# A graph layer's node windows sized by their place in the sorted edges, with fifteen segments in place of thirty-three

## The chip, the cores and the metric

The kernel runs on one core of a Trainium2 chip. The metric is the device time of one execution in microseconds (us). The engines are named as in the profile: PE (TensorE matmul, with PEld for its weight loads), DVE (VectorE), ACT (ScalarE), POOL (GpSimd) and SP (SyncE, which here issues DMAs only). Times inside an execution are given in us from the start of its span.

## What is computed

One message-passing layer over 12,500 nodes of 48 features and 400,000 edges of 32 features, sorted by destination:

```python
h = jnp.maximum(_layernorm(x, axis=-1), 0.0)
x_i = h[dst]
x_j = h[src]
tmp = jnp.concatenate([x_i, x_j, edge_attr], axis=1)
hid = jax.nn.relu(tmp @ W1 + b1)
msg = hid @ W2 + b2
out = jax.ops.segment_sum(msg, dst, num_segments=12500)
return x + out
```

`W1` is 128 by 128, `W2` is 128 by 48, all in float32. `dst` is drawn as 12500 times the square of a uniform number and then sorted, so the low nodes have many edges each and the high nodes few: a run of 1,024 edges covers few nodes at the start and some tens at the end.

## The kernel before

**Tables first.** `node_tables` (up to about 75 us) normalises the nodes and multiplies them by the two node parts of `W1`. It writes `tab_a` (for destinations) and `tab_b` (for sources) to DRAM and leaves the normalised rows turned in `ht`. It also computes a flag that sends the kernel to another path, `general`, if the edges of some chunk cover too many nodes; with these inputs the path is `windows`.

**Chunks.** `windows` walks the edges in 391 chunks of 8 tiles of 128 edges. The nodes of a chunk lie in a window that starts at the chunk's first destination and is `W` = 80 nodes wide. For chunk c:

- `prepare(c)`: SP loads the edge features into rows 80 to 111 of `lhs`, the destinations broadcast to 80 partitions (`row`), and 80 rows of `tab_a` (`rhs`). POOL gathers the source rows of `tab_b` into `gb` by one indirect DMA for each tile, for those tiles that come in no other way. DVE compares `row` with the window's node numbers, which fills rows 0 to 79 of `lhs` with a 0/1 matrix and sums the degrees into `deg` (L379).
- `columns(c, part)`: some tiles come as columns. A turned copy of the source table (`bt`) is kept in SBUF, and DVE (71) and ACT (72) copy one 128x1 column for each edge into `gt` (L348), at addresses that are loaded into registers (L272).
- `rows`: 15 rows for each chunk come into `gs` by small DMAs of SP (L289).
- `compare(c)`: DVE makes the 0/1 matrix `hot`, 128 edges by 8 tiles by 80 nodes (L389).
- `before(c)` multiplies `lhs` with `rhs` into `pre` (L400); `gathered(c)` adds the source rows to it (L421); `hidden(c)` is the relu on ACT (L437).
- `fold(c)` multiplies `hid` with `hot` into `p_g`, 8 tiles one after another (L445), and turns the degrees (L448); `add(c)` adds `p_g` into the running segment `seg` at the window's place (L460).

The first four chunks have their source rows gathered from x itself (`xg`), so POOL's gathers into `gb` start with chunk 4. Of a chunk's eight tiles POOL gathers 7 as a rule, sometimes 6: 2,618 gathers in all.

**Segments.** `seg` is one of two buffers of 1,024 nodes. Twelve chunks share a segment (`GQ`; the first has four, and the last three). At a segment's end `segment_next` clears the other buffer (L476, two memsets) and copies the overlap of 80 nodes into it (L478, SBUF to SBUF). In the chunks that follow, `segment_sum` multiplies the old segment by `W2` and `b2` in two halves of 512 nodes (L488, L489), `segment_add` adds them to `xseg` (L495), and `segment_store` writes it (L499).

**Order.** All engines run a hand-written order (`manual_schedule`): in round c the loop does `prepare(c)`, `before(c-1)`, `fold(c-2)`, `add(c-2)`, `compare(c)`, `gathered(c-1)`, `hidden(c-1)`, with `columns` in between and the segment's work near the end of the round. POOL has nothing but its gathers in this loop. It runs ahead of the others until `gb` has no free buffer: the pool `gp` has 7, and a chunk's buffer comes free when PE has read it in L421.

Of the kernel before, what the change touches and what calls it, by code (L numbers as in the profile page):

```python
# [8 lines left out]
F32 = mybir.dt.float32  # L9
I32 = mybir.dt.int32  # L10
AF = mybir.ActivationFunctionType
ALU = mybir.AluOpType
# [30 lines left out]
RAW_PART = 16  # L43
HALF = (W - 1) / 2
K = W + DE
# [27 lines left out]
BT0 = 16512  # L73
SEG0 = 161696
SEG_SIZE = 8 * L
# [154 lines left out]
def windows(nc, tc, gp, bt, ident, idx, raw, rhss, x_t, tab_a, tab_b, dst, edge_t, w2s, b2s,  # L230
# [5 lines left out]
    with ExitStack() as es:  # L236
# [15 lines left out]
        wnum = ps_w.tile([P, W], F32, name="wnum")  # L252
        nc.vector.tensor_scalar_add(wnum, wrow, -HALF)

# [8 lines left out]
        def group(c):  # L263

            return divmod(c + OFF, GQ)

        def begin(g):
            return max(0, g * GQ - OFF)

# [55 lines left out]
        def columns(c, part):  # L325
# [15 lines left out]
            for k, of in enumerate(got[:n]):  # L341
# [6 lines left out]
                copy(gts[j][:, e : e + 1], bt8[:, bass.ds(of, 4)].bitcast(F32))  # L348

        def prepare(c):  # L350
            n = min(T, NT - c * T)
            at = c * CE
            lhs = ld.tile([P, CE], F32, name="lhs")
# [10 lines left out]
            nc.sync.dma_start(  # L364
                rhs.bitcast(U8)[:W, :],
                taba8[bass.ds(base, 4 * HID * W)].rearrange("(w h) -> w h", w=W),
            )
# [11 lines left out]
            nc.vector.tensor_scalar(  # L379
                lhs[:W, : n * P], row[:, : n * P], bw[:, c : c + 1], None,  # L380
                op0=ALU.is_equal, op1=ALU.add, accum_out=deg[:, :1],
            )
            st[c].update(rhs=rhs, lhs=lhs, gb=gb, deg=deg)

        def compare(c):

            n = st[c]["n"]
            hot = wp.tile([P, T, W], F32, name="hot")
            nc.vector.tensor_tensor(  # L389
                hot[:, :n, :], wnum.unsqueeze(1).to_broadcast([P, n, W]),  # L390
                rel[:, c * T : c * T + n].unsqueeze(2).to_broadcast([P, n, W]), op=ALU.is_equal,
            )
            st[c]["hot"] = hot
# [46 lines left out]
        def fold(c):  # L440
            s = st[c]
            n = s["n"]
            p_g = ps_g.tile([HID, 2, W], F32, name="p_g")
            for t in range(n):
                nc.tensor.matmul(  # L445
                    p_g[:, 0, :], s["h"][:, t, :], s["hot"][:, t, :], start=t == 0, stop=t == n - 1
                )
            nc.tensor.matmul(p_g[:, 1, :], s["deg"], ident[:W, :W], start=True, stop=True)  # L448
            s["p_g"] = p_g

        def add(c):

            s = st.pop(c)
# [6 lines left out]
            nc.vector.tensor_add(to, to, s["p_g"])  # L460
# [3 lines left out]
        def segment_load(g):  # L464

            first, = numbers(begin(g), SEG, 1, mybir.EngineType.SP)
            xs[g] = xp.tile([D, L], F32, name="xseg")
            n = L if begin(g + 1) < NCH else END_L
            nc.sync.dma_start(xs[g][:, :n], x_t[:, bass.ds(node(first), n)])

# [26 lines left out]
        def segment_store(g, n):  # L497
            first, = numbers(begin(g), SEG, 1, mybir.EngineType.SP)
            nc.sync.dma_start(out_t[:, bass.ds(node(first), n)], xs.pop(g)[:, :n])  # L499

        with tc.manual_schedule():
            for c in range(NCH + 2):
# [30 lines left out]
                columns(c, 10)  # L533
                if k == GQ - 3 or c == NCH - 1:
# [21 lines left out]
def general(nc, tc, bt, ident, x_t, tab_a, tab_b, src_it, dst_it, dst, edge_t, w1, w2s, b2s,  # L556
            accs, out_t):

    with ExitStack() as es:
# [97 lines left out]
        with tc.tile_pool(name="gfin", bufs=1) as fin, tc.tile_pool(  # L657
            name="g_f", bufs=1, space=PSUM
        ) as ps_f:
            for r0 in range(0, NR, 14):  # L660
                s = slice(r0, r0 + 14)
                got = []
                for k in range(GNACC):
                    a = fin.tile([P, 14, D], F32, name=f"a{k}")
                    nc.sync.dma_start(
# [5 lines left out]
                nc.vector.tensor_add(got[0], got[0], got[2])  # L671
                for r in range(14):
                    p_f = ps_f.tile([D, P], F32, name="p_f")
# [6 lines left out]
def tile_gnn_preln(  # L680
# [63 lines left out]
    for k in range(3):  # L744
        deg = const.tile([W, P], F32, name=f"deg{k}")
        nc.gpsimd.memset(deg, 0.0)
        degs.append(deg)
    gp = ctx.enter_context(tc.tile_pool(name="gp", bufs=7))

    with tc.tile_pool(name="keep", bufs=1) as keep, tc.tile_pool(  # L750
# [14 lines left out]
        def loads():  # L765
# [12 lines left out]
            gather(0, RAW_PART)  # L778
            nc.gpsimd.tensor_scalar_add(b0f, b0f, HALF)
            full = NT // T  # L780
# [18 lines left out]
        def squares():  # L799
            nc.scalar.activation(bt[:, :NT], rel, AF.Square)  # L800

        def sources():

            nc.sync.dma_start(srci[:, FIRST:], src_cols[:, FIRST:])

        furthest = keep.tile([P, 1], F32, name="furthest")
        widest = keep.tile([P, 1], F32, name="widest")
# [3 lines left out]
        def most():  # L811
# [3 lines left out]
            )  # L815
            nc.vector.tensor_scalar(furthest, furthest, HALF * HALF, None, op0=ALU.is_gt)
            nc.vector.tensor_scalar(widest, widest, MID * MID, None, op0=ALU.is_gt)
            nc.vector.tensor_tensor(furthest, furthest, widest, op=ALU.max)

        def check():  # L820
# [6 lines left out]

            nc.vector.tensor_scalar_add(wcol, wcol, -HALF)
            nc.vector.tensor_scalar(bw, b0f[:W, :], wcol[:W, :], None, op0=ALU.add)
# [105 lines left out]
```

## Time and profile before

| | |
|---|---|
| median of three executions | 3366.36 us (3366.21 to 3367.52) |
| the profiled execution's own time | 3372.65 us |
| its span, first to last instruction | 3370.8 us |
| mean granted TensorE clock | 0.911 |
| busy | PE 82%, PEld 64%, DVE 83%, ACT 90%, POOL 75% |
| moved by DMA | 349.24 MB, 104 GB/s in the mean |

The trace's numbers are those of the profiled execution, and sums are made against its span. A line such as "3353.48 0.95 POOL L371 ... [0.30 <-issue]" is a row of the timeline: start, duration, engine, line, operation, operands and count, then the engine's idle time just before and what ended it. In the groups by line, the two numbers behind the bar are the busy time in us and the mean duration in ns, and behind the second bar stands the idle time before these instructions.

### The profile page before, as it was taken

To read this page: it belongs to the slowest core of one execution; us is meant where nothing else is said; L and a number is where in the kernel's file an instruction comes from. 1 tells how busy PE (TensorE), PEld (TensorE's weight loads), DVE (VectorE), ACT (ScalarE), POOL (GpSimd) and SP (SyncE) were. 2 spreads that over 40 slices of the span, in tenths; PEclk is the share of its full clock that TensorE was granted. 3 is DMA by queue.
4 is the path that set the end of the run, shared out by engine and by line. 5 is a ranking of instruction groups with operands and counts; after the bars stand their busy time and mean duration, and the time that the engine had idled before them with its cause. 6 is when DMAs were issued, how large, how long until landed. Compare 5 with 4: busy or idle time off the path is not lost.

```text
span 3370.8 us, 115212 instructions
## 1 busy us (share of the span) xinstructions
PE 2775.6 (82%) x16394; PEld 2158.3 (64%) x16394; DVE 2800.1 (83%) x29140; ACT 3035.6 (90%) x28179; POOL 2530.0 (75%) x2670
## 2 busy tenths in 40 slices
PE   7987778888888888888887788888788788788777
PEld 6666666666666666666666666676666666666565
DVE  6588888888888888888888888888888888888876
ACT  5799998999998999998899999889998999999987
POOL 7677777777777777777777777777777777777776
PEclk9999998998898998988889999888998999899989
DMA  7433333333333333333333333333333333333333
GB/s 262 122 97 104 100 97 100 99 101 100 100 99 100 95 100 102 100 101 97 100 98 101 100 100 102 95 101 97 102 99 98 97 100 98 104 100 97 99 96 83
DMA packets 200234, 349.24 MB, mean 104 GB/s; under 512 B 69219, under 2 KB 107749, under 8 KB 198181
## 3 DMA queue, kind: packets, MB, share of 16 engines
q0 software_dynamic: 84800, 172.53, 18.9%
q1 hardware_dynamic: 114258, 169.09, 16.7%
q14 instruction: 634, 5.19, 0.5%
q8 instruction: 138, 2.26, 0.3%
q10 hardware_dynamic: 404, 0.17, 0.0%
HBM read 322.05 MB, written 22.07 MB: 102 GB/s over the span
## 4 chain that ended last, share of the span: by engine, by line
DVE 71%; issue 14%; PE 5%; DVEq 4%; POOL 2%; DMA 2%; ACT 0%; SPq 0%; POOLq 0%; ACTq 0%
DVE gt L348 47%; DVE lhs L379 12%; DVE hot L389 8%; DVEq L272 4%; DVE seg L460 2%; POOL gb L371 2%; PE pre L400 1%; PE p_g L445 1%; DVE xseg L495 1%; DVE seg L476 1%; DMA row<-in_dst 1%; PE p_f L488 1%; PE p_f L489 1%; DMA gb<-tab_b,srci 1%; PE p_n L195 1%
## 5 line engine op out<-in xcount | busy, mean ns | idle before, releaser
L371 POOL DMA_INDIRECT gb<-tab_b,srci x2618 | 2489.4, 951 | 812.7 <-issue 724.4
L348 ACT COPY gt<-bt 128x1 f32 x27705 | 2618.0, 188 | 63.9 <-issue 54.6
L348 DVE COPY gt<-bt 128x1 f32 x27335 | 1842.1, 144 | 463.3 <-issue 435.1
L400 PEld LDWEIGHTS pre<-rhs,lhs 112*128 112x128 f32 x6250 | 823.5, 208 | 277.1 <-issue 193.4
L400 PE MATMUL pre<-rhs,lhs 112*128 112x128 f32 x6250 | 841.5, 292 | 98.3 <-issue 56.7
L445 PE MATMUL p_g<-hot,hid 128*128 128x80 f32 x6250 | 794.0, 282 | 131.2 <-ACT hid L437 129.1
L445 PEld LDWEIGHTS p_g<-hot,hid 128*128 128x128 f32 x6250 | 758.4, 198 | 164.4 <-ACT hid L437 161.6
L421 PE MATMUL pre<-gb,ident 128*128 128x512 f32 (+2 forms) x1548 | 771.2, 627 | 34.3 <-DMA gb<-tab_b,srci 26.5
L437 ACT ACTIVATE hid<-pre 128x1024 f32<-128x1024 f32 x391 | 397.5, 1017 | 220.2 <-PE pre L421 205.8
L379 DVE TENSOR_SCALAR_CACHE_REDUCE lhs<-row,bw 80x1024 f32<-80x1024 int16 x391 | 494.6, 1265 | 14.8 <-DMA row<-in_dst 14.5
L421 PEld LDWEIGHTS pre<-gb,ident 128*128 128x128 f32 x1548 | 311.8, 225 | 281.0 <-issue 261.7
L421 PE MATMUL pre<-ident,gt 128*128 128x128 f32 x860 | 214.9, 336 | 261.7 <-DVE gt L348 234.7
L421 PEld LDWEIGHTS pre<-ident,gt 128*128 128x128 f32 x860 | 143.8, 210 | 291.5 <-issue 136.4
L389 DVE TENSOR_TENSOR hot<-wnum,rel 128x640 f32<-128x640 f32 x391 | 318.2, 814 | 0.0
L460 DVE TENSOR_TENSOR seg<-seg,p_g 128x160 f32 x391 | 121.5, 311 | 47.8 <-PE p_g L448 47.8
L448 PE MATMUL p_g<-ident,deg 80*128 80x80 f32 x782 | 156.4, 283 | 0.0
L448 PEld LDWEIGHTS p_g<-ident,deg 80*128 80x128 f32 x782 | 123.6, 198 | 0.0
L488 PE MATMUL p_f<-seg,w2s 128*48 128x512 f32 (+1 forms) x134 | 82.2, 700 | 44.3 <-DVE xseg L495 43.9
L489 PE MATMUL p_f<-seg,b2s 1*48 1x512 f32 (+1 forms) x134 | 76.2, 650 | 0.0
L488 PEld LDWEIGHTS p_f<-seg,w2s 128*48 128x48 f32 x134 | 12.3, 135 | 85.9 <-DVE xseg L495 60.0
L476 DVE MEMSET seg<- 128x944 f32 x64 | 54.1, 845 | 9.3
L489 PEld LDWEIGHTS p_f<-seg,b2s 1*48 1x48 f32 x134 | 11.3, 122 | 65.2 <-issue 65.2
(76 smaller groups left out, 429.0 us busy)
## 6 DMA issues: line engine op xcount, KB each, us to landing
gs<-tab_b SPq DMA_DIRECT2D x5760, 0.5 KB
row<-in_dst SPq DMA_DIRECT2D x390, 160.0 KB
lhs<-in_edge_t SPq DMA_DIRECT2D x390, 128.0 KB
gb<-tab_b,srci POOLq DMA_INDIRECT x2618
rhs<-tab_a SPq DMA_DIRECT2D x391, 40.0 KB
xseg<-in_x_t SPq DMA_DIRECT2D x33, 192.0 KB
out_x<-xseg SPq DMA_DIRECT2D x33, 192.0 KB
tab_b<-tab SPq DMA_DIRECT2D x3, 1280.0 KB
```

Source lines behind the costliest of these rows:

```text
L272: return nc.values_load_multi_w_load_instructions(table[c % P : c % P + 1, c // P, at : at + n], engines=[engine], min_val=0, max_val=1 << 23,
L348: copy(gts[j][:, e : e + 1], bt8[:, bass.ds(of, 4)].bitcast(F32))
L371: nc.gpsimd.indirect_dma_start(out=gb[:, t, :], out_offset=None, in_=tab_b[:, :], in_offset=bass.IndirectOffsetOnAxis(ap=srci[:, c * T + t ...
L379: nc.vector.tensor_scalar(lhs[:W, : n * P], row[:, : n * P], bw[:, c : c + 1], None, op0=ALU.is_equal, op1=ALU.add, accum_out=deg[:, :1],)
L389: nc.vector.tensor_tensor(hot[:, :n, :], wnum.unsqueeze(1).to_broadcast([P, n, W]), rel[:, c * T : c * T + n].unsqueeze(2).to_broadcast([P ...
L400: nc.tensor.matmul(pre[:, t, :], s["lhs"][:K, t * P : (t + 1) * P], s["rhs"][:K, :], start=t % BANK == 0, stop=False, skip_group_check=True,)
L421: nc.tensor.matmul(pre[:, t:e, :], lhsT, rhs, start=False, stop=True, skip_group_check=True)
L437: nc.scalar.activation(h[:, :n, :], s["pre"][:, :n, :], AF.Relu)
L445: nc.tensor.matmul(p_g[:, 0, :], s["h"][:, t, :], s["hot"][:, t, :], start=t == 0, stop=t == n - 1)
L448: nc.tensor.matmul(p_g[:, 1, :], s["deg"], ident[:W, :W], start=True, stop=True)
L460: nc.vector.tensor_add(to, to, s["p_g"])
L488: nc.tensor.matmul(p_f[:, :n], w2s, seg[:, 0, s], start=True, stop=False)
```

## The change

The window's width depends on the chunk's place: 16 nodes for chunks 0 to 77, 32 to chunk 164, 48 to 249, 64 to 339, and 80 for the rest. The broadcast of the destinations, the rows of `tab_a`, both comparisons, the columns of `hot` in the fold, the turned degrees and the add into the segment are that wide. `lhs` becomes three fixed buffers whose node rows are cleared once by DVE (and those of `rhs` by POOL), since the matmul L400 still contracts over all 112 rows. Window numbers count from 0 instead of from the window's middle, which removes two small additions of `HALF` (one on POOL), and the check's squares are made in five pieces. `gp` gets 8 buffers. Segments begin at fixed chunks: fifteen of them, the first of 103 chunks, the last of five with a final sum of 400 nodes instead of 320. `xseg` has one buffer and the last segment its own; a segment is stored one round later than before, except the one before the last. The columns stay 71 for DVE and 72 for ACT, and the gathers stay 2,618. The rest of the diff is smaller tiles in `general`.

```diff
-GQ = 12
-OFF = -(NCH - 3) % GQ
+BEGINS = (0, 103, 147, 180, 208, 233, 255, 275, 294, 312, 329, 345, 360, 374, NCH - 5)
-END_L = 4 * W
+END_L = 5 * W
-STORE = 2
+STORE = 3
-HALF = (W - 1) / 2
+SPANS = ((16, 78), (32, 165), (48, 250), (64, 340), (W, NCH))
...
+        lhss = [one.tile([P, CE], F32, name=f"lhs{k}") for k in range(3)]
+        for lhs in lhss:
+            nc.vector.memset(lhs[:W, :], 0.0)
...
+        wh = es.enter_context(tc.tile_pool(name="wh", bufs=2))
-        xp = es.enter_context(tc.tile_pool(name="xp", bufs=2))
+        xp = es.enter_context(tc.tile_pool(name="xp", bufs=1))
...
+        def span(c):
+            return next(w for w, last in SPANS if c < last)
...
             nc.sync.dma_start(
-                row[:, : n * P],
-                dst[at : at + n * P].rearrange("(o e) -> o e", o=1).to_broadcast([W, n * P]),
+                row[:w, : n * P],
+                dst[at : at + n * P].rearrange("(o e) -> o e", o=1).to_broadcast([w, n * P]),
             )
...
             nc.vector.tensor_scalar(
-                lhs[:W, : n * P], row[:, : n * P], bw[:, c : c + 1], None,
-                op0=ALU.is_equal, op1=ALU.add, accum_out=deg[:, :1],
+                lhs[:w, : n * P], row[:w, : n * P], bw[:w, c : c + 1], None,
+                op0=ALU.is_equal, op1=ALU.add, accum_out=deg[:w, :1],
             )
...
-            hot = wp.tile([P, T, W], F32, name="hot")
+            hot = wh.tile([P, T * W], F32, name="hot")
+            hot = hot[:, : T * w].rearrange("p (t w) -> p t w", w=w)
...
-            p_g = ps_g.tile([HID, 2, W], F32, name="p_g")
+            p_g = ps_g.tile([HID, 2 * W], F32, name="p_g")
+            p_g = p_g[:, : 2 * w].rearrange("h (k w) -> h k w", k=2)
...
-            to = segs[k].bitcast(U8)[:, :, bass.ds(at, 4 * W)].bitcast(F32)
+            to = segs[k].bitcast(U8)[:, :, bass.ds(at, 4 * w)].bitcast(F32)
...
-                    if k == GQ - 1:
+                    if c - 1 == begin(g + 1) < NCH:
                         segment_next(g)
...
-                if g > 0 and k == STORE:
+                if g > 0 and k == (STORE if begin(g + 1) < NCH else 2):
                     segment_store(g - 1, L)
...
+    for rhs in rhss:
+        nc.gpsimd.memset(rhs[:W, :], 0.0)
-    gp = ctx.enter_context(tc.tile_pool(name="gp", bufs=7))
+    gp = ctx.enter_context(tc.tile_pool(name="gp", bufs=8))
...
-            nc.gpsimd.tensor_scalar_add(b0f, b0f, HALF)
...
-            nc.scalar.activation(bt[:, :NT], rel, AF.Square)
+            at = 0
+            for k, (w, last) in enumerate(SPANS):
+                to = min(NT, last * T)
+                nc.scalar.activation(
+                    bt[:, at:to], rel[:, at:to], AF.Square,
+                    bias=shift[:, k : k + 1], scale=1.0 / reach(w),
+                )
+                at = to
```

Two places show how instructions move. The first is DVE at the end of the second segment of the kernel before, in the round that adds chunk 15: the add into the segment, then the memsets and the copy of the overlap.

```order
L460 TENSOR_TENSOR seg_635<-seg_635,p_g 128x2x80
L476 MEMSET seg_634 128x944 x2
L272 TENSOR_LOAD last
L478 ISA
L478 COPY seg_634<-seg_635 128x2x80
```

In the change DVE goes from one add straight on to the next columns here, and this group stands 14 times in the program instead of 33 (its first copy without the memsets in both). At the same place:

```order
L471 TENSOR_TENSOR seg_645<-seg_645,p_g 128x2x16
L276 TENSOR_LOAD cols
L352 COPY gt<-bt 128x1 x16
L398 TENSOR_TENSOR hot<-wnum,rel 128x128
L276 TENSOR_LOAD cols
```

The second place is the end of PE's queue in the kernel before, from the source rows of the chunk before the last; `x5` is the last chunk, which has five tiles.

```order
L421 MATMUL pre<-gb,ident 128x384
L488 MATMUL p_f<-seg_634,w2s 48x512
L489 MATMUL p_f<-seg_634,b2s 48x512
L400 MATMUL pre<-rhs_89,lhs 128x128 x5
L445 MATMUL p_g<-hot,hid 128x80 x8
L448 MATMUL p_g<-ident,deg_99 128x80
L421 MATMUL pre<-gb,ident 128x512
L421 MATMUL pre<-gb,ident 128x128
L488 MATMUL p_f<-seg_634,w2s 48x512
L489 MATMUL p_f<-seg_634,b2s 48x512
L445 MATMUL p_g<-hot,hid 128x80 x5
L448 MATMUL p_g<-ident,deg_95 128x80
```

The same stretch of the change has no sums of the segment before the last in it. They stand behind the source rows of the two chunks before, since the last segment now has five chunks:

```order
L430 MATMUL pre<-gb,ident 128x384
L409 MATMUL pre<-rhs_89,lhs_653 128x128 x5
L456 MATMUL p_g<-hot,hid 128x80 x8
L459 MATMUL p_g<-ident,deg_102 128x80
L430 MATMUL pre<-gb,ident 128x512
L430 MATMUL pre<-gb,ident 128x128
L456 MATMUL p_g<-hot,hid 128x80 x5
L459 MATMUL p_g<-ident,deg_98 128x80
```

Behind both stand only the last segment's sums, 320 columns wide before and 400 now.

More of the change, by code (lines that the diff above doesn't have):

```diff
@@ L263, in group @@
         def group(c):
-            return divmod(c + OFF, GQ)
+            g = max(0, sum(first <= c for first in BEGINS) - 1)
+            return g, c - BEGINS[g]
         def begin(g):
-            return max(0, g * GQ - OFF)
+            return BEGINS[g] if g < len(BEGINS) else NCH
         def numbers(c, at, n, engine, table=last):
@@ L385, in compare @@
         def compare(c):
-            n = st[c]["n"]
-            hot = wp.tile([P, T, W], F32, name="hot")
+            n, w = st[c]["n"], span(c)
+            hot = wh.tile([P, T * W], F32, name="hot")
+            hot = hot[:, : T * w].rearrange("p (t w) -> p t w", w=w)
             nc.vector.tensor_tensor(
-                hot[:, :n, :], wnum.unsqueeze(1).to_broadcast([P, n, W]),
-                rel[:, c * T : c * T + n].unsqueeze(2).to_broadcast([P, n, W]), op=ALU.is_equal,
+                hot[:, :n, :], wnum[:, :w].unsqueeze(1).to_broadcast([P, n, w]),
+                rel[:, c * T : c * T + n].unsqueeze(2).to_broadcast([P, n, w]), op=ALU.is_equal,
             )
@@ L447, in fold @@
                 )
-            nc.tensor.matmul(p_g[:, 1, :], s["deg"], ident[:W, :W], start=True, stop=True)
+            nc.tensor.matmul(p_g[:, 1, :], s["deg"], ident[:W, :w], start=True, stop=True)
             s["p_g"] = p_g
         def add(c):
-            s = st.pop(c)
+            s, w = st.pop(c), span(c)
             k = group(c)[0] % 2
@@ L659, in general @@
         ) as ps_f:
-            for r0 in range(0, NR, 14):
-                s = slice(r0, r0 + 14)
+            for r0 in range(0, NR, 7):
+                s = slice(r0, r0 + 7)
                 got = []
                 for k in range(GNACC):
-                    a = fin.tile([P, 14, D], F32, name=f"a{k}")
+                    a = fin.tile([P, 7, D], F32, name=f"a{k}")
                     nc.sync.dma_start(
@@ L671, in general @@
                 nc.vector.tensor_add(got[0], got[0], got[2])
-                for r in range(14):
+                for r in range(7):
                     p_f = ps_f.tile([D, P], F32, name="p_f")
@@ L878 @@
     first = dst[::CE]
-    of = (np.arange(NCH) + OFF) // GQ
-    seg = first[np.maximum(of * GQ - OFF, 0)]
-    nxt = first[np.minimum(of * GQ - OFF + GQ, NCH - 1)]
+    of = np.searchsorted(BEGINS, np.arange(NCH), side="right") - 1
+    seg = first[np.array(BEGINS)[of]]
+    nxt = first[np.array(BEGINS[1:] + (NCH - 1,))[of]]
     numbers[2 : NCH + 2, AT_SEG] = seg
```

31 lines of the change are left out of this document (18 added, 13 removed).

## The prediction

> **What bounds the kernel now.** I read the chain of waits first, then the groups by line, the windows and POOL's timeline.
>
> ```profile
> DVE 71%; issue 14%; PE 5%; DVEq 4%; POOL 2%; DMA 2%; ACT 0%; SPq 0%; POOLq 0%; ACTq 0%
> ...
> L371 POOL DMA_INDIRECT gb<-tab_b,srci x2618 | 2489.4, 951 | 812.7 <-issue 724.4
> L348 ACT COPY gt<-bt 128x1 f32 x27705 | 2618.0, 188 | 63.9 <-issue 54.6
> L348 DVE COPY gt<-bt 128x1 f32 x27335 | 1842.1, 144 | 463.3 <-issue 435.1
> L437 ACT ACTIVATE hid<-pre 128x1024 f32<-128x1024 f32 x391 | 397.5, 1017 | 220.2 <-PE pre L421 205.8
> L379 DVE TENSOR_SCALAR_CACHE_REDUCE lhs<-row,bw 80x1024 f32<-80x1024 int16 x391 | 494.6, 1265 | 14.8 <-DMA row<-in_dst 14.5
> L389 DVE TENSOR_TENSOR hot<-wnum,rel 128x640 f32<-128x640 f32 x391 | 318.2, 814 | 0.0
> L460 DVE TENSOR_TENSOR seg<-seg,p_g 128x160 f32 x391 | 121.5, 311 | 47.8 <-PE p_g L448 47.8
> ```
>
> The chain names DVE, but POOL's gathers with the idle time before them fill 2489.4 + 812.7 = 3302.1 us of the span, nearly all of what lies between the first and the last of them, and that idle time is issue. The windows and the timeline show that this stream hardly ever pauses:
>
> ```profile
> 1500.00:1900.00 400.00, 337.18 (x1968) 263.30 (x1966) 338.50 (x3601) 368.99 (x3494) 302.67 (x320) 0.89 0.35 99
> ...
> 52.62 0.95 POOL L371 DMA_INDIRECT gb<-tab_b,srci  x1 [0.34 <-issue]
> ...
> 100.14 0.95 POOL L371 DMA_INDIRECT gb<-tab_b,srci  x1 [0.30 <-issue]
> ...
> 113.90 0.95 POOL L371 DMA_INDIRECT gb<-tab_b,srci  x1 [0.30 <-issue]
> 127.82 0.95 POOL L371 DMA_INDIRECT gb<-tab_b,srci  x1 [12.98 <-PE pre L421]
> ...
> 161.48 0.95 POOL L371 DMA_INDIRECT gb<-tab_b,srci  x1 [1.45 <-PE pre L421]
> ...
> 3353.48 0.95 POOL L371 DMA_INDIRECT gb<-tab_b,srci  x1 [0.30 <-issue]
> ```
>
> In a stage of 400 us POOL (the fifth pair) has 320 gathers, one each 1.25 us. From 52.62 to 113.90 are 49 steps of 1.2506 us, 50 gathers: chunks 4 to 10, which fill seven buffers. POOL then stands until PE has read chunk 4. From 127.82 to 3353.48 are 2,567 steps in 3225.7 us; at 1.2506 they would take 3210.3, so 15.4 us are lost in 3.2 ms. DVE and ACT are just quick enough: ACT needs 2618.0 + 63.9 + 397.5 = 3079 us for 391 chunks, 7.9 each, where POOL needs 2618 x 1.2506 / 387 = 8.46. So POOL's stream is the bound, with what lies ahead of it, its pauses, and a tail of 3370.8 - 3354.4 = 16.4 us.
>
> **What takes the 15.4 us.** Waits for a buffer are few after the one at 161.48, which lost 1.15. Most of it is gathers that last longer, and these stand at the segments' ends:
>
> ```profile
> L371 POOL DMA_INDIRECT gb<-tab_b,srci x2618: 940/947/1924, 52.6 to 3353.5; - x187
> ...
> 827.93 1.84 DVE L476 MEMSET seg<- 128x944 f32 x2
> 828.85 1.83 POOL L371 DMA_INDIRECT gb<-tab_b,srci  x1 [0.30 <-issue]
> 829.69 0.18 DVE L478 COPY seg<-seg 128x160 f32 x1
> ...
> 3241.89 1.22 POOL L371 DMA_INDIRECT gb<-tab_b,srci  x1 [0.30 <-issue]
> ...
> 80.50 1.76 DVE L522 MEMSET seg<- 128x2048 f32 x1 [0.37 <-issue]
> ...
> 81.37 0.94 POOL L371 DMA_INDIRECT gb<-tab_b,srci  x1 [0.31 <-issue]
> ```
>
> The copy L478 ends at 829.87, inside a gather, and the gather ends 0.81 later, at 830.68, as if begun anew. A memset alone does not do this: the one at 80.50 leaves the gather at 81.37 at 0.94. Of the 32 copies after the first wait 22 fall into a gather and lengthen it, the last at 3241.89, by 13.7 us in all (the timeline's durations over the median of 0.947; the longest is 1.924). That is 0.43 for each copy.
>
> The Trainium skill (SBUF — State Buffer, "SBUF: two separate sides") says that a DVE instruction in a two-port mode, such as a float32 copy inside SBUF, locks GpSimd out of a shared port, so that it can't write its descriptors until DVE lets go. [...]
>
> **The change, part by part, on POOL's path.**
>
> Gathers: 2,618 as before. Their step doesn't hang on how busy DVE is (1.2509 us from 100.14 to 113.90, eleven steps while DVE waits; 1.2506 while it is busy): nothing.
>
> Eighth buffer: POOL goes on with chunk 11's six gathers before it waits for chunk 4, and reaches chunk 12 at 52.62 + 56 x 1.2506 = 122.65. Chunk 4 is released at 127.8 as before, if the start keeps its pace. Gain 6 x 1.2506 = 7.5 us; bounds: 12.7 if PE comes 5.2 us earlier, 4.5 if it comes 3 later.
>
> The start: DVE's three memsets of 1,024 columns cost about 0.9 each (1.76 us for the 2,048 above).
>
> ```profile
> L800 ACT ACTIVATE bt<-rel 128x3125 f32<-128x3125 f32 x1 | 2.8, 2813 | 0.0
> L779 POOL TENSOR_SCALAR b0f<-b0f 128x391 f32<-128x391 f32 x1 | 1.2, 1223 | 0.1
> ...
> 78.11 1.27 DVE L379 TENSOR_SCALAR_CACHE_REDUCE lhs<-row,bw 80x1024 f32<-80x1024 int16 x1 [7.68 <-DMA row<-in_dst]
> ```
>
> DVE stands 7.68 us there, which covers them; uncovered they are 2.7. The five squares add perhaps 0.7 on ACT, and POOL saves 1.2 of L779; both end in POOL's wait for chunk 4. I take 0, with -1 to +3.
>
> Segment copies: 14 instead of 33, at 0.43: 6.0 instead of 13.7, gain 7.7. Bounds: 0 (none hits a gather) to 13 (each costs the most seen, 0.93). The other pauses, 1.7 us with the one at 161.48, fall to about 0.5, since the first segment now ends far behind it and a buffer is worth 8.75 us: gain 1.2.
>
> DVE's own work: `hot` took 814 ns for 640 elements, `add` 311 for 160. A last chunk of 400 elements gives a slope:
>
> ```profile
> L389 DVE TENSOR_TENSOR hot<-wnum,rel 128x400 f32<-128x400 f32 x1 | 0.6, 564 | 0.0
> ...
> L495 DVE TENSOR_TENSOR xseg<-xseg,p_f 48x512 f32<-48x512 f32 (+1 forms) x67 | 44.7, 667 | 8.5 <-PE p_f L489 8.5
> ```
>
> (814 - 564) / 240 = 1.04 ns. The windows lose 34 columns in the mean (64 x 78 + 48 x 87 + 32 x 85 + 16 x 90, over 391), so `hot` saves 8 x 34 x 1.04 = 283 ns and `add` 2 x 34 x 1.04 = 71 for each chunk, 138 us; L379 has the same 1,024 columns on fewer partitions and saves nothing; 18 fewer segment ends save 18 x (1.84 + 0.18 + 2 x 0.667) = 60. That is 198 us of DVE, 0.5 a chunk, but DVE is not what POOL waits for. On the path: 0. The same holds for the smaller loads, for PE, and for SP, whose waits at the stores run ahead of need; if none of it were covered, it would already show as waits of POOL.
>
> Tail:
>
> ```profile
> 3323.47 0.95 POOL L371 DMA_INDIRECT gb<-tab_b,srci  x1 [0.30 <-PE p_g L448]
> ...
> 3326.23 0.70 PE L421 MATMUL pre<-gb,ident 128*128 128x256 f32 x2 [1.37 <-DMA gb<-tab_b,srci]
> ...
> 3352.91 1.94 PE L488 MATMUL p_f<-seg,w2s 128*48 128x512 f32 x2
> 3354.78 1.12 PE L489 MATMUL p_f<-seg,b2s 1*48 1x512 f32 x2
> 3359.02 1.28 PE L421 MATMUL pre<-gb,ident 128*128 128x512 f32 x4
> 3360.40 0.70 ACT L437 ACTIVATE hid<-pre 128x640 f32<-128x640 f32 x1 [6.30 <-PE pre L421]
> 3361.22 1.05 PE L489 MATMUL p_f<-seg,b2s 1*48 1x512 f32 x2
> 3362.21 1.34 PE L445 MATMUL p_g<-hot,hid 128*128 128x80 f32 x10
> 3364.19 0.74 PE L488 MATMUL p_f<-seg,w2s 128*48 128x320 f32 x2 [0.41 <-DVE seg L460]
> ```
>
> A gather lands 1.8 us after its end (3324.42, read at 3326.23). The last ends at 3354.43, but PE reads it at 3359.02, held by the old segment's first sums. Those move two chunks ahead, so PE can read it at about 3356.4: 2.6 saved. The second pair stood between `hid`'s end (3361.1) and the last fold (3362.21): 1.1 saved. Sums of 400 columns instead of 320 cost a quarter of two matmul groups of 0.74, and DVE's add 0.1: 0.5 lost. Gain 3, between 0 and 5.
>
> Sum: 7.5 + 7.7 + 1.2 + 3 = 19.4 us off the span: 3351.4. The span of the profiled run lies 4.4 us above the median of the runs shown (3370.8 to 3366.4), so the forecast is **3347 us**; its own range, by the copies' luck and the bounds of start and tail, is 3342 to 3353.
>
> **Rivals.**
>
> (a) PE comes to chunk 4 earlier, because the fold with 16 columns is quicker.
>
> ```profile
> 138.01 1.87 PEld L445 LDWEIGHTS p_g<-hot,hid 128*128 128x128 f32 x16
> 138.12 1.91 PE L445 MATMUL p_g<-hot,hid 128*128 128x80 f32 x16
> ...
> 123.82 1.75 PE p_g L445 x16
> ```
>
> Four folds lie on the chain before chunk 4's release. If each lost 1.3 us, POOL would no longer wait at all: 5.2 more, 3342. Against it: the 16 weight loads alone take 1.87 of the 1.91 us, and they stay. The Trainium skill (TensorE: Matmul & The Clock Gate, "Back-to-back issue gap") has an isolated gap that falls with the moving columns to about 60 cycles at 64 and fewer; by that this rival wins. The same section says that in a stream of loads and matmuls both set the pace, which is what the rows show. 12%.
>
> (b) The start slips by about 3 us, the copies hit often and the tail gains nothing: 3347 + 3 + 5 + 3 = 3358. Each alone is within its bound, all together are unlikely. 9%.
>
> (c) DVE is the bound, as the chain says. Then its 198 us come off: 3366 - 198 = 3168. For it: the chain's 71%. Against it: POOL's step of 1.2506 that no DVE load changes. 2%.
>
> (d) Slower: a narrowed DVE instruction takes the fast copy's path and breaks gathers as L478 does. L379 or L389 with 16 to 64 columns runs in each chunk; at 0.43 for each of 387 chunks the loss is 166 us: 3347 + 166 = 3513. It decides from 45 hits on, 19.4 / 0.43. For it: such breaks exist, and only the operation's form tells which do it. Against it: L379 at 1265 ns and L389 at 814 run at over 1 ns an element and break nothing now, and the types and memories of both stay. 5%.
>
> (e) The gain is eaten by something that no row shows, to within 0.2%: 2%.
>
> **How the numbers follow.** About 0.2% (6.7 us) is what a measurement of this kernel can tell from no change. The forecast has 70%. Faster takes it with (a), (c) and most of (b), whose upper end reaches no change: 0.90; within 0.2%, the rest of (b) and (e): 0.04; slower, (d) and a share of what I have not seen: 0.06. The range reaches from (a), with 2 us for the tail's bound, to most of (b): 3340 to 3356.
>
> **What would show it.** In the profile after: 2,618 gathers with a step of 1.25 us; one long wait of POOL near 122 to 128 us of 4 to 6 instead of 12.98; long gathers only at about ten segment copies, 5 to 7 us in sum; DVE's `hot` near 280 ns with 16 columns and L379 unchanged at 1265; DVE busy near 2,600 us with the time hardly changed; 13 to 14 us between the last gather's end and the span's. Wrong would be: gathers of 1.3 us and more in each chunk, waits of POOL for PE after 200 us, or a POOL stream that ends early while PE goes on.

## The result, and the profile after

The changed kernel takes 3348.14 us (median of 5 runs, 3345.56 to 3351.62), the kernel before 3367.47 in the same comparison (3366.21 to 3371.47). The ratio is 0.9942, with a 95% interval of 0.9927 to 0.9956: 19.3 us less, beyond what this measurement can tell from no change. The forecast was 3347, in a range of 3340 to 3356. The profiled run took 3348.55 us, its span is 3346.8. Six of the runs below come from a second chip, on which the kernel before, too, takes about 1.6 times as long; they are told apart from the rest.

The page of the changed kernel, with the busy times, the chain of waits and the groups that answer to those shown of before:

```profile
span 3346.8 us, 114800 instructions
...
PE 2804.1 (84%) x16242; PEld 2228.4 (67%) x16242; DVE 2608.9 (78%) x29052; ACT 3044.9 (91%) x28183; POOL 2516.1 (75%) x2672
...
DVE 34%; POOL 25%; issue 22%; PE 10%; ACT 4%; DMA 3%; DVEq 2%; ACTq 0%; SPq 0%; POOLq 0%
...
L379 POOL DMA_INDIRECT gb<-tab_b,srci x2618 | 2476.4, 946 | 805.3 <-issue 759.8
L352 DVE COPY gt<-bt 128x1 f32 x27335 | 1839.8, 143 | 616.7 <-issue 578.7
L430 PE MATMUL pre<-gb,ident 128*128 128x512 f32 (+2 forms) x1548 | 851.7, 668 | 234.9 <-DMA gb<-tab_b,srci 227.7
L456 PE MATMUL p_g<-hot,hid 128*128 128x64 f32 (+4 forms) x6250 | 789.9, 279 | 111.2 <-ACT hid L446 109.2
```

DVE is busy for 191 us less (2800.1 before), and the time fell by a tenth of that. The chain, which gave POOL 2% before, now gives it 25%, and PE's source-row matmuls stand 227.7 us waiting for a gather to land (26.5 before). The gathers with the idle time before them fill 2476.4 + 805.3 = 3281.7 us: the stream is as dense as before, only shorter. Its timeline (start and duration in us, then the idle time before and what ended it) has one long wait and the long gathers, eleven in all, of which the first, the longest and the last are shown:

```profile
52.58 0.94 POOL L379 DMA_INDIRECT gb<-tab_b,srci  x1 [1.77 <-issue]
...
121.25 0.94 POOL L379 DMA_INDIRECT gb<-tab_b,srci  x1 [0.30 <-issue]
128.07 0.94 POOL L379 DMA_INDIRECT gb<-tab_b,srci  x1 [5.88 <-PE pre L430]
...
1288.03 1.57 POOL L379 DMA_INDIRECT gb<-tab_b,srci  x1 [0.30 <-issue]
...
2678.91 1.77 POOL L379 DMA_INDIRECT gb<-tab_b,srci  x1 [0.30 <-issue]
2678.93 0.84 DVE L487 MEMSET seg<- 128x944 f32 x1
...
2679.69 0.18 DVE L489 COPY seg<-seg 128x160 f32 x1
...
3303.33 1.73 POOL L379 DMA_INDIRECT gb<-tab_b,srci  x1 [0.30 <-issue]
...
3331.58 0.94 POOL L379 DMA_INDIRECT gb<-tab_b,srci  x1 [0.30 <-issue]
```

From these the 24.0 us between the two spans (3370.8 and 3346.8) can be laid out. A step is the time from one gather's start to the next, taken as the mean of all steps that hold no long gather and no wait.

| part of POOL's path | before | after | gain, us |
|---|---|---|---|
| first gather | 52.62 | 52.58 | 0.0 |
| the one long wait, over a plain step | 12.67 | 5.57 | 7.1 |
| long gathers at segment copies | 22, 13.7 | 11, 5.8 | 7.9 |
| all other pauses | 1.2 | 0.0 | 1.2 |
| the plain step, 2,617 times | 1.2508 | 1.2486 | 5.7 |
| end of the last gather to the end | 16.4 | 14.3 | 2.1 |

The step is the only part that the forecast does not have as such. What was taken off there for the profiled execution, 4.4 us over its median, is of its size. That the parts add up to the whole is bookkeeping; what each is worth in time, the experiments have to show.

### The profile page after: what moved, and what is told of

It reads as the page before. It is cut to its first block, busy times and chain, and to the rows that moved or that the text cites. A ratio compares the mean times of both kernels' runs of the same rounds, so it can differ in the third digit from the quotient of the medians.

```text
span 3346.8 us, 114800 instructions
## 1 busy us (share of the span) xinstructions
PE 2804.1 (84%) x16242; PEld 2228.4 (67%) x16242; DVE 2608.9 (78%) x29052; ACT 3044.9 (91%) x28183; POOL 2516.1 (75%) x2672
## 4 chain that ended last, share of the span: by engine, by line
DVE 34%; POOL 25%; issue 22%; PE 10%; ACT 4%; DMA 3%; DVEq 2%; ACTq 0%; SPq 0%; POOLq 0%
POOL gb L379 25%; DVE gt L352 25%; DVE lhs L387 6%; ACT gt L352 3%; DMA gb<-tab_b,srci 3%; PE pre L409 3%; PE pre L430 2%; PE p_g L456 2%; DVE hot L398 2%; DVEq L276 2%; PE p_n L194 1%; ACT hid L446 1%; DVE seg L471 1%; PE pre L306 0%; ACTq L276 0%
## 5 line engine op out<-in xcount | busy, mean ns | idle before, releaser
L379 POOL DMA_INDIRECT gb<-tab_b,srci x2618 | 2476.4, 946 | 805.3 <-issue 759.8
L352 ACT COPY gt<-bt 128x1 f32 x27705 | 2619.5, 188 | 76.6 <-issue 66.1
L352 DVE COPY gt<-bt 128x1 f32 x27335 | 1839.8, 143 | 616.7 <-issue 578.7
L430 PE MATMUL pre<-gb,ident 128*128 128x512 f32 (+2 forms) x1548 | 851.7, 668 | 234.9 <-DMA gb<-tab_b,srci 227.7
L409 PEld LDWEIGHTS pre<-rhs,lhs 112*128 112x128 f32 x6250 | 888.6, 220 | 187.0 <-issue 118.4
L409 PE MATMUL pre<-rhs,lhs 112*128 112x128 f32 x6250 | 884.3, 302 | 27.5 <-issue 17.1
L456 PE MATMUL p_g<-hot,hid 128*128 128x64 f32 (+4 forms) x6250 | 789.9, 279 | 111.2 <-ACT hid L446 109.2
L387 DVE TENSOR_SCALAR_CACHE_REDUCE lhs<-row,bw 64x1024 f32<-64x1024 int16 (+4 forms) x391 | 492.2, 1259 | 3.0 <-DMA row<-in_dst 3.0
L398 DVE TENSOR_TENSOR hot<-wnum,rel 128x512 f32<-128x512 f32 (+4 forms) x391 | 207.0, 529 | 0.0
L459 PE MATMUL p_g<-ident,deg 80*128 80x32 f32 (+4 forms) x782 | 159.7, 286 | 0.0
L471 DVE TENSOR_TENSOR seg<-seg,p_g 128x128 f32 (+4 forms) x391 | 94.1, 241 | 80.6 <-PE p_g L459 79.9
L499 PE MATMUL p_f<-seg,w2s 128*48 128x512 f32 (+1 forms) x58 | 35.9, 705 | 5.5 <-DVE xseg L506 5.1
L500 PE MATMUL p_f<-seg,b2s 1*48 1x512 f32 (+1 forms) x58 | 33.3, 656 | 0.0
L203 ACT COPY tab<-p_n 128x512 f32<-128x512 f32 x33 | 18.7, 584 | 12.1 <-PE p_n L194 11.8
L387 DVE DVE_READ_ACCUMULATOR lhs<-row,bw 64x1 f32 (+4 forms) x391 | 28.8, 74 | 0.0
```

The costliest lines, as they stand in the source:

```text
L379: nc.gpsimd.indirect_dma_start(out=gb[:, t, :], out_offset=None, in_=tab_b[:, :], in_offset=bass.IndirectOffsetOnAxis(ap=srci[:, c * T + t ...
L387: nc.vector.tensor_scalar(lhs[:w, : n * P], row[:w, : n * P], bw[:w, c : c + 1], None, op0=ALU.is_equal, op1=ALU.add, accum_out=deg[:w, :1],)
L398: nc.vector.tensor_tensor(hot[:, :n, :], wnum[:, :w].unsqueeze(1).to_broadcast([P, n, w]), rel[:, c * T : c * T + n].unsqueeze(2).to_broad ...
L409: nc.tensor.matmul(pre[:, t, :], s["lhs"][:K, t * P : (t + 1) * P], s["rhs"][:K, :], start=t % BANK == 0, stop=False, skip_group_check=True,)
L430: nc.tensor.matmul(pre[:, t:e, :], lhsT, rhs, start=False, stop=True, skip_group_check=True)
L456: nc.tensor.matmul(p_g[:, 0, :], s["h"][:, t, :], s["hot"][:, t, :], start=t == 0, stop=t == n - 1)
```

## The experiments

The first four ran side by side with the kernel before (3367.55 us median of 14). They take back or alter one part of the change at a time.

**Seven buffers instead of eight** (the segments' tile moves by the 4,096 bytes that come free):

```diff
-    gp = ctx.enter_context(tc.tile_pool(name="gp", bufs=8))
+    gp = ctx.enter_context(tc.tile_pool(name="gp", bufs=7))
```

> The change with seven gather buffers instead of eight, nothing else. Theory (POOL's gather stream sets the time): POOL stops before chunk 11 again and waits about 13 us for chunk 4; six gathers of 1.249 us are lost: 3348.1 + 7.5 = 3355.6 us (3353.5 to 3357.5). Rival (the time comes from DVE's lighter work, the buffer only moves a wait): 3348, since DVE's work is the same.

Measured: 3354.91 us (3350.68 to 3358.51), ratio 0.9958 [0.9943, 0.9972], 6.8 us over the changed kernel. POOL's timeline in this run:

```profile
115.12 0.94 POOL L379 DMA_INDIRECT gb<-tab_b,srci  x1 [0.30 <-issue]
130.12 0.94 POOL L379 DMA_INDIRECT gb<-tab_b,srci  x1 [14.05 <-PE pre L430]
```

The wait stands one chunk earlier, 8.2 us longer, and no second one follows; long gathers cost 5.6 us, as in the change. The buffer is worth one chunk of gathers, once.

**The old segments** (with all else as in the change; they are 34, one of four chunks, 32 of twelve and one of three, and the thirty-three of the heading are the copies between them):

```diff
-BEGINS = (0, 103, 147, 180, 208, 233, 255, 275, 294, 312, 329, 345, 360, 374, NCH - 5)
+BEGINS = (0,) + tuple(range(4, NCH, 12))
```

> The change with the segments of before (first of four chunks, then twelve each, a last of three). Theory: 32 segment copies after the first wait instead of 14, each 0.43 to 0.50 us in the mean, cost 18 x 0.46 = 8.3 us more, and the old segment's sums stand in the tail again, 2 to 3 us: 3348.1 + 10.8 = 3359 (3355 to 3362). Rival (segment ends cost only DVE time, which is covered): 3348 to 3351, the tail alone.

Measured: 3358.24 us (3357.15 to 3365.18), ratio 0.9969 [0.9959, 0.9978], 10.1 us over the change. Again 22 of the copies fall into gathers and lengthen them, now by 12.5 us where the change has 5.8. So the segments are the larger half of the gain, as the sum had it (7.7 for the copies, 1.2 and 3 for what hangs on the segments besides).

**All windows 80 columns wide:**

```diff
-SPANS = ((16, 78), (32, 165), (48, 250), (64, 340), (W, NCH))
+SPANS = ((W, NCH),)
```

> The change with every window 80 nodes wide, segments and buffers as in the change. Theory (POOL's stream; DVE is not on the path): DVE is busy 138 us longer, the time stays: 3348 (3346 to 3350). Rival 1 (DVE is the bound, as the chain of waits before said): 3348 + 138 = 3486. Rival 2 (a busier DVE stretches each gather's step, which was 1.2508 us before and 1.2486 after): the step goes back to 1.2508, 2561 x 0.0022 = 5.6 us: 3354.

Measured: 3349.53 us (3348.56 to 3350.1), ratio 0.9943 [0.9928, 0.9958]. The page and the groups of this run:

```profile
PE 2705.8 (81%) x16242; PEld 2152.8 (64%) x16242; DVE 2749.9 (82%) x29048; ACT 3041.7 (91%) x28179; POOL 2519.1 (75%) x2672
...
L352 DVE COPY gt<-bt 128x1 f32 x27335 | 1841.9, 144 | 479.5 <-issue 444.4 <-ACT gt L352 1.5 <-ACT bt L311 1.2
L456 PE MATMUL p_g<-hot,hid 128*128 128x80 f32 x6250 | 788.9, 281 | 101.6 <-ACT hid L446 99.5 <-issue 0.7
```

DVE has 141 us of work back (2749.9 against 2608.9), and the time rises by 1.4, inside the spread of the change's own runs. That the two are so close has some luck in it: in this profile the plain step is 1.2505 us, which costs 4.9 us over the change's, and fewer long gathers (4.6 us instead of 5.8) and a shorter tail (11.8 instead of 14.3) give 3.7 of it back. The step of the second rival did come, then, but not from DVE's load: the run with the old segments has 1.2505 with DVE at 2662.7 us, and the last run below has 1.2485 with 80-column windows and DVE at 2922.0. What is added to DVE's busy time leaves its idle time: the issue idle before the column copies falls by 134 us, 578.7 to 444.4. A fold's matmul takes 281 ns here and 279 in the mean over the change's five widths. The part of the change with the most lines in the diff has no measurable share in its gain.

**The overlap copied by ACT** (with the register that its place is read from; the memsets stay on DVE):

```diff
-            of, = numbers(begin(g), NEXT, 1, mybir.EngineType.DVE)
-            nc.vector.tensor_copy(
+            of, = numbers(begin(g), NEXT, 1, mybir.EngineType.Activation)
+            nc.scalar.copy(
```

> The change with the overlap's copy at a segment's end on ACT instead of DVE, nothing else. Theory (DVE's copy inside SBUF breaks the gather under way, and no other segment work does): no long gathers are left, 6 to 7 us come off: 3341.5 (3340 to 3343.5). Rival (the memsets of 944 columns, or anything else at a segment's end, break the gathers): long gathers stay, 3348.

Measured: 3342.59 us (3339.91 to 3343.74), ratio 0.9925 [0.9910, 0.9939]: the fastest version of this study. The tile view (minimum, median and maximum in ns) and the timeline at a memset:

```profile
L379 POOL DMA_INDIRECT gb<-tab_b,srci x2618: 940/944/961, 52.4 to 3325.2; - x187
...
1289.53 0.84 DVE L487 MEMSET seg<- 128x944 f32 x1
...
1290.02 0.94 POOL L379 DMA_INDIRECT gb<-tab_b,srci  x1 [0.30 <-issue]
```

No gather is over 961 ns any more, where the change had 1,774, and a gather inside a memset keeps its 0.94. This shows that it takes DVE's copy to lengthen them, since nothing else was changed, and that the memsets alone do not. (Not every copy of DVE does it; see the last section.) The 5.8 us are gone from the trace and 5.6 from the time.

The next six ran on the slow chip, four beside a kernel before of 5326.64 us and two beside one of 5406.67. The first four were to tell whether the step of 1.2486 belongs to the program or to the execution, and to relieve POOL. `b_again` and `a_again` are the kernel before and the change with nothing altered, one run each; the other two gather at most six tiles of a chunk, and the rest of its matmuls take the sixth tile's rows, so that 286 gathers and what their rows add are left out:

```diff
-            for t in range(n - len(COLS_OF.get(c, ())) - (c in BYROWS) if c >= RAW else 0):
+            own = n - len(COLS_OF.get(c, ())) - (c in BYROWS) if c >= RAW else 0
+            for t in range(own if c < 16 else min(6, own)):
...
```

> The kernel before once more, for a second profile. Open is whether the step of a gather (1.2508 us in the first profile of before, 1.2486 in the change) belongs to the kernel or to the execution. If to the kernel: 1.2508 again. If to the execution: anything between 1.248 and 1.251, with the time moving by 2.6 us for each 0.001.

> The change once more, for a second profile. If the step belongs to the kernel: 1.2486 again and a span near 3347. If to the execution: it can be 1.2505 as in two of the four variants of the change, and the span is then near 3352.

> The kernel before with at most six gathers in a chunk from chunk 16 on (the seventh tile takes the sixth tile's rows, so 286 tiles of source rows are wrong). Theory: POOL then needs 7.5 us a chunk and is no longer the bound; DVE, with (2740 + 463) / 391 = 8.2 us a chunk of work and issue, is next: 128 + 386 x 8.2 = 3293 us (3260 to 3325). Rival (DVE, ACT or PE is the bound already): the time stays at 3367.

> The change with at most six gathers in a chunk from chunk 16 on (the same 286 tiles take wrong rows). Theory: POOL is no longer the bound, DVE needs 0.5 us a chunk less than in the kernel before, and ACT is next with (2618 + 64 + 398) / 391 = 7.9 us a chunk: 128 + 386 x 7.95 = 3197 us (3180 to 3245), so the change is worth 60 to 110 us there, not 19. Rival (DVE's lighter work is worth nothing anywhere): the distance to the kernel before stays at 19.

Measured: `b_again` 5316.56 us, `a_again` 5409.47; `b_six` 5036.25 (ratio 0.9453 [0.9435, 0.9472]) and `a_six` 5100.0 (0.9569 [0.9543, 0.9595]) against the kernel before on that chip. The question of the step has an answer in `b_again`. Its first gather and its fiftieth:

```profile
68.25 0.94 POOL L371 DMA_INDIRECT gb<-tab_b,srci  x1 [16.20 <-DMA tab_b<-tab]
...
129.40 0.94 POOL L371 DMA_INDIRECT gb<-tab_b,srci  x1 [0.30 <-issue]
```

These are 49 steps of (129.40 - 68.25) / 49 = 1.2480 us, where the same kernel's first profile has 1.2506 over the same stretch (52.62 to 113.90). Over all plain steps `b_again` and `a_again` both have 1.2481. So the program alone does not fix the step; whether the chip or the single execution does, these runs can't part. What POOL's stream is worth they do not answer, as the groups of `a_again` show:

```profile
L352 ACT COPY gt<-bt 128x1 f32 x27705 | 2900.5, 187 | 1718.0 <-issue 1698.9 <-ACT gt L352 1.4 <-remote 1.1
L379 POOL DMA_INDIRECT gb<-tab_b,srci x2618 | 2472.5, 944 | 2816.5 <-PE pre L430 1773.5 <-issue 727.3 <-PE pre L409 146.5
L352 DVE COPY gt<-bt 128x1 f32 x27335 | 2019.8, 143 | 2123.4 <-issue 2096.0 <-ACT bt L311 1.9
```

A column copy lasts what it lasts on the other chips (143 and 187 ns), but ACT and DVE stand idle before them for 1699 and 2096 us with no releaser, 66.1 and 578.7 in the change's own profile, and POOL waits 1773.5 us for PE. Where POOL is not the bound, a shorter POOL stream is no test of it; that both kernels are 4 to 5% faster there with six gathers is not explained. Nor is it explained that the change is behind the kernel before on this chip, by one run each (5409.47 and 5316.56) and by four runs each with six gathers (5100.0 and 5036.25). The gain of 19 us is thus not shown for the slow chip.

The other two had ACT's overlap copy and 24 gathers fewer, by eight more column copies a chunk, on both engines or on DVE alone (the second one's list of parts stands below):

```diff
-    (True, 0, 8), (True, 8, 15), (True, 24, 16), (True, 40, 20), (True, 60, 12),
+    (True, 0, 8), (True, 8, 15), (True, 24, 16), (True, 40, 20), (True, 60, 16),
...
-    (False, 132, 12),
+    (False, 136, 16),
...
```

> The change with the overlap's copy on ACT and eight more columns a chunk, four on DVE (75) and four on ACT (76): 2594 gathers instead of 2618. Theory: one gather less before the first wait counts for nothing, 23 behind it give 23 x 1.2486 = 28.7 us, if ACT's 8.2 us a chunk still fit under POOL's 8.37: 3342.6 - 28.7 = 3314 (3310 to 3320). Rival (ACT becomes the bound): nothing is gained, 3335 or more.

> The change with the overlap's copy on ACT and eight more columns a chunk, all on DVE (79, ACT keeps 72): 2594 gathers. Theory: DVE has about 0.7 us a chunk free in the change, and eight columns with their loads cost it 0.55 to 0.65: 3314 (3310 to 3322). Rival (DVE is the bound in the last stages, where the windows are 64 and 80 nodes wide): 3322 to 3340.

Measured: 5613.95 us (ratio 1.0379 [1.0365, 1.0393]) and 5578.71 (1.0321 [1.0306, 1.0335]). The column copies come late on this chip, and the runs say nothing of the theory. The second was therefore run again, and beside it the same kernel with 80-column windows. Both landed on a chip where the kernel before takes 3368.16 us (median of 9):

```diff
-    (True, 0, 8), (True, 8, 15), (True, 24, 16), (True, 40, 20), (True, 60, 12),
+    (True, 0, 8), (True, 8, 15), (True, 24, 20), (True, 44, 20), (True, 64, 16),
...
```

> The changed kernel with the overlap columns copied by ACT instead of DVE, and eight more columns of each tile made by DVE's column copies (79 by DVE and 72 by ACT), so that 23 gathers fewer are left (2,595 of 2,618). Theory (POOL's gather stream is the bound, DVE has room): 3342.6 for the version with ACT's copy alone, less 23 x 1.2486 = 28.7: 3314 (3308 to 3320). Rival (DVE's own work per chunk now sets the pace): about 7.0 us of DVE's work per chunk on average after the change is far under the 8.37 us of a chunk's gathers, but in the last chunks, 64 and 80 columns wide, it would be near 8.5, and the time would come to 3325 to 3345.

> As the run beside it, with all windows 80 columns wide (the narrow windows of the change taken back). Theory (DVE's time per chunk matters only where it passes that of the chunk's gathers, 8.3 to 8.4 us): the 80-column chunk costs DVE about 0.36 us more on the mean, 141 us in all as in the earlier run with windows of 80, which puts DVE's busy time near 2,800 us of 3,314; so the windows are still hidden, or nearly: 3314 to 3325. Rival (DVE, with its issue time of about a fifth beside its busy time, is the bound at full width): it falls behind in every chunk, and the time is 3335 to 3420.

Measured: 3596.23 us (3595.97 to 3599.36), ratio 1.0673 [1.0654, 1.0693], and 3597.0 (3596.94 to 3600.3), ratio 1.0674 [1.0655, 1.0694]. Both have 2,594 gathers (the first expectation counts 2,595). Every time expected of the first is wrong by 251 us or more, of the second by 177 or more; the side on which the rival stood (DVE sets the pace) is the right one, far more strongly than it said. First the run with narrow windows, then the one with wide ones:

```profile
PE 2892.1 (80%) x16290; PEld 2322.4 (65%) x16290; DVE 2781.8 (77%) x32118; ACT 3051.8 (85%) x28189; POOL 2487.1 (69%) x2648
...
DVE 72%; issue 20%; PE 3%; DVEq 3%; ACT 1%; DMA 0%; ACTq 0%; SPq 0%
...
L352 DVE COPY gt<-bt 128x1 f32 x30415 | 2016.8, 144 | 735.6 <-issue 721.4
...
1500.64 1.06 DVE L352 COPY gt<-bt 128x1 f32 x16 [0.55 <-issue]
...
1505.44 1.42 DVE L352 COPY gt<-bt 128x1 f32 x20 [0.92 <-issue]
...
1507.94 1.30 DVE L352 COPY gt<-bt 128x1 f32 x20 [0.75 <-issue]
```

```profile
PE 2800.3 (78%) x16290; PEld 2257.9 (63%) x16290; DVE 2922.0 (81%) x32114; ACT 3050.7 (85%) x28185; POOL 2486.8 (69%) x2648
...
L352 DVE COPY gt<-bt 128x1 f32 x30415 | 2018.3, 144 | 600.1 <-issue 561.1
...
1506.67 1.30 DVE L352 COPY gt<-bt 128x1 f32 x20 [0.46 <-issue]
```

No engine is over 85% busy, and yet the kernel is 7% slower. In the first run DVE hardly waits for another engine any more (34.6 us for PE before its adds, in 7 waits, where the change has 79.9 in 32), while POOL, which in the change has one long wait, stands 257.3 us for PE, in 154 waits. DVE goes from one chunk's L387 to the next in (3576.8 - 79.5) / 390 = 8.97 us in the first run and (3578.3 - 78.5) / 390 = 8.97 in the second; in the change it is (3328.5 - 78.3) / 390 = 8.33, POOL's pace (first and last start of L387 by the line view):

```profile
L387 DVE TENSOR_SCALAR_CACHE_REDUCE lhs<-row,bw x391: 864/1259/1270, 79.5 to 3576.8; 64x1024 f32<-64x1024 int16 x45, 32x1024 f32<-32x1024 int16 x44, 48x1024 f32<-48x1024 int16 x42, 16x1024 f32<-16x1024 int16 x39
```

The 140 us of busy time between the two runs leave the pace as it is: they are taken out of the idle time before the column copies (721.4 and 561.1 us). So what sets the pace there is not how long DVE's instructions run. The pieces are five a chunk as in the change; what grew is the number of column copies in them, 30,415 instead of 27,335. Why these bring idle time with them, and what the idle time marked as issue consists of, was not tried.

## Why the prediction was right, step by step

- **The bound.** Right for this change. What shows it is POOL's stream: behind its one wait no gather of the change stands longer than the 0.3 us that lie before each, and the runs that alter only POOL's pauses (seven buffers, ACT's copy) move the time by what POOL loses or gains. DVE's 191 us (198 were reckoned, with 18 segment ends fewer where it is 19) came off without a gain, and the rival by which they come off the time, 3168, falls. The run with 80-column windows would not have shown this alone: the last pair has equal times too, although DVE sets the pace there. "Just quick enough" was truer than its numbers. DVE's busy time and the issue idle before its copies come to about (2608.9 + 578.7) / 391 = 8.15 us a chunk in the change, against POOL's 8.33, and eight more column copies a chunk put DVE in front.
- **Eighth buffer, 7.5.** 7.1 in the profile, 6.8 us in time when it is taken back. POOL's long wait ends at 128.07 as it did at 127.82 before, so the start cost next to nothing (0 was taken, of -1 to +3).
- **Segment copies, 7.7, and other pauses, 1.2.** 7.9 and 1.2. Eleven of 14 copies hit, at 0.53 each, where two of three at 0.62 had been seen; the sum per copy, 0.42, is the 0.43 of before. That the copy is needed for it, until then read off one instant, is shown by the run with ACT's copy. The Trainium skill (SBUF — State Buffer, "SBUF: two separate sides") says that a float32 copy within SBUF on DVE locks GpSimd out of a port that the two share, and that ACT never waits on anyone there. The runs agree in part: DVE's copy behind the memsets lengthens a gather, ACT's does not, but a copy that DVE began after a pause did not either (last section). They disagree with the size: by the same section of the Trainium skill the other engine is blocked until DVE's end and about 115 ns more, here an estimate of at most 0.30 us with a copy of 0.18, and the gather lost up to 0.83.
- **Tail, 3.** 2.1: a term mis-sized, in this execution. The prediction let PE begin on the last chunk's rows 2.0 us after the last gather's end; it begins 3.2 us after. The tail's timeline in the changed kernel, from the last gather on:

```profile
3331.58 0.94 POOL L379 DMA_INDIRECT gb<-tab_b,srci  x1 [0.30 <-issue]
...
3333.63 2.01 PE L456 MATMUL p_g<-hot,hid 128*128 128x80 f32 x16
...
3335.70 1.28 PE L430 MATMUL pre<-gb,ident 128*128 128x512 f32 x4
...
3337.84 1.34 PE L456 MATMUL p_g<-hot,hid 128*128 128x80 f32 x10 [0.85 <-ACT hid L446]
...
3339.82 0.87 PE L499 MATMUL p_f<-seg,w2s 128*48 128x400 f32 x2 [0.41 <-DVE seg L471]
```

  The segment's sums are out of the way as forecast, but the fold of the chunk before stands ahead of the rows in PE's queue as well (the listing of the change has it there) and begins only at 3333.63: 4.6 us from the gather's end to PE's read became 3.2, not 2.0. From the read to the end, 11.8 became 11.1, the 0.6 that was reckoned. This hangs on how late PE is at the end. With the same order in the queue, the profiles with ACT's copy and with 80-column windows have tails of 11.9 and 11.8 us; there the fold is done in time and PE waits for a gather to land, as in this row of the run with ACT's copy:

```profile
3326.55 1.74 PE L430 MATMUL pre<-gb,ident 128*128 128x512 f32 x4 [0.67 <-DMA gb<-tab_b,srci]
```

- **The step.** "Nothing" was the forecast. It is 1.2486 where the kernel before had 1.2508, 5.7 us in all. It is constant within an execution from the first gathers on. The change, seven buffers and ACT's copy all have 1.2486; the kernel before, the wide windows and the old segments 1.2508, 1.2505 and 1.2505. It is no gain of the change that anything here shows: the kernel before has 1.2481 in its second profile, on the slow chip, and the change has 1.2481 there too. The 4.4 us that were taken off because the profiled execution lay above its median come to nearly the same, so the forecast of 3347 does not hang on it.
- **Rival (a), a quicker fold.** It falls. At 16 columns a matmul of the fold takes 265 ns instead of 282, and chunk 4 is not released earlier:

```profile
L456 PE MATMUL p_g<-hot,hid 128*128 128x16 f32 x1248 | 154.2, 265 | 26.4 <-ACT hid L446 26.0
...
137.34 1.86 PE L456 MATMUL p_g<-hot,hid 128*128 128x16 f32 x16
```

  A fold of 16 takes 1.86 us here and took 1.91 before, where the rival needs 1.3 less. The Trainium skill (TensorE: Matmul & The Clock Gate, "Back-to-back issue gap") says that in a stream of weight loads and matmuls both set the spacing. This case agrees: a fifth of the columns shortens it by 6% (265 ns against 281, at granted clocks near 0.85 and 0.91), so the weight loads, which stay, hold it up. **(b)** did not come: the start kept its time and the copies their price. **(d)** falls: no gather but those at copies is long, with the windows at 16 columns as at 80.

## What to carry to other kernels

Find the stream that never pauses, write down each of its pauses with its price, and count what the change does to these; 141 us of work taken off another engine were worth 1.4 here. But a busy share of 78% is no reserve: eight more small copies a chunk made DVE the bound, with 7% lost, so idle time marked as issue has to be counted as the engine's time until a run shows otherwise. A copy of 0.18 us that DVE made right behind its memsets, beside a stream of POOL's gathers, cost 0.42 us in the mean, and on ACT nothing.

## What the runs showed of the hardware that was not expected

The granted clock of TensorE falls with the narrow windows. These are three stages (to 1500, to 2900 and to 3300 us) of the changed kernel, with the clock as the first number behind the five engines' busy times:

```profile
100.00:1500.00 1400.00, 1202.04 (x7000) 967.28 (x6999) 1069.01 (x12690) 1316.09 (x12349) 1054.07 (x1117) 0.85 0.31 81
1500.00:2900.00 1400.00, 1162.92 (x6774) 918.80 (x6772) 1120.44 (x12484) 1283.53 (x12091) 1059.14 (x1119) 0.88 0.34 90
2900.00:3300.00 400.00, 323.14 (x1935) 256.93 (x1934) 333.29 (x3551) 366.13 (x3448) 302.40 (x321) 0.91 0.38 100
```

And the same stages with all windows at 80:

```profile
100.00:1500.00 1400.00, 1138.80 (x6978) 919.20 (x6976) 1163.10 (x12648) 1309.58 (x12305) 1054.43 (x1116) 0.91 0.37 98
1500.00:2900.00 1400.00, 1126.71 (x6778) 892.79 (x6779) 1162.32 (x12484) 1286.14 (x12118) 1058.89 (x1119) 0.91 0.37 98
2900.00:3300.00 400.00, 323.87 (x1916) 253.18 (x1916) 332.04 (x3544) 364.40 (x3432) 302.68 (x320) 0.90 0.37 99
```

In the first stage the windows are 16 and 32 columns wide, in the second 48 and 64, in the third 80: 0.85, 0.88, 0.91. With wide windows it stays at 0.90 to 0.91 throughout. PE has the same 16,242 matmuls in both and is busy for 98 us longer with the narrower ones (2804.1 and 2705.8), its source-row matmuls above all (851.7 us, 781.4 with wide windows). The pair with 79 columns shows it again, 0.844 and 0.878. Why fewer columns bring a lower clock, the runs do not show; here PE has room for it.

The other finding is how much a copy of 0.18 us costs POOL. The gather at 2678.91 would have ended at 2679.85; the copy that began at 2679.69 ended at 2679.87, and the gather at 2680.68, 0.81 later. The price hangs on when in the gather the copy comes; in the change it is between 0.17 and 0.83 us. In all 33 lengthened gathers of the two kernels (22 and 11) it is the time that the gather had already run when the copy began, plus 0.04 to 0.06 us, so the gather takes its whole time once more.

Each of these 33 copies stands straight behind its memsets. The first copy of a program has no memsets ahead of it, and in the change it falls into a gather and leaves it alone (first two rows); so do the first copies in the runs with seven buffers and with 80-column windows. On the slow chip DVE made one copy 1.37 us after its memsets, again within a gather, and that gather is not lengthened either (last two rows, of `a_again`):

```profile
928.43 0.95 POOL L379 DMA_INDIRECT gb<-tab_b,srci  x1 [0.31 <-issue]
929.07 0.36 DVE L489 COPY seg<-seg 128x160 f32 x1
...
3891.20 0.95 POOL L379 DMA_INDIRECT gb<-tab_b,srci  x1 [0.30 <-issue]
3891.98 0.24 DVE L489 COPY seg<-seg 128x160 f32 x1 [1.37 <-DVE seg L487]
```

So neither the memset nor the copy alone lengthens a gather in these profiles, only the copy that follows the memset without a pause. Why, and whether a pause would do as well as ACT, was not tried.
